# Three ordering products of a lattice stretch, moved from one quadrant of the array to three

## The chip, the core and the metric

The kernel runs on one core of a Trainium2 chip. The metric is the device time of one execution in microseconds; of the kernel before there are three timed runs, 12310.65, 12336.9 and 12346.97 us, with the median 12336.9 us. The engines that matter here are TensorE (PE in the profile; its weight loads have a row of their own, PEld), VectorE (DVE), ScalarE (ACT), GpSimd (POOL), and the DMA queue that SyncE (SP) issues.

## The reference, cut to what matters

The input x is 32 images of 8 channels of 256 by 256 values, fp32. Layer 0 normalises each image over groups of two channels and then computes three things from the result: a coupled map lattice, a small cellular network and a gate that blends the two. Layer 1 is a quantised 3x3 convolution. Each layer is added to its input. The lattice, which the change touches, is this part:

```python
drive = x[:, :C_OUT]
grid = drive
for _ in range(STEPS):                       # STEPS = 15
    mapped = R * grid * (1.0 - grid)         # R = 3.9
    local = _conv(mapped, K_local, groups=C_OUT)   # 3x3, each channel by itself
    physics = (1.0 - EPS) * mapped + EPS * local
    grid = (1.0 - BETA) * physics + BETA * drive
cml_out = jnp.clip(grid, 0.0001, 1.0 - 0.0001)
```

The network is a 3x3 convolution from 8 to 128 channels, a relu and a 1x1 convolution back to 8 with a sigmoid. The gate is a 3x3 convolution of 24 channels to 8, a relu, a 1x1 convolution and a sigmoid. Layer 1 needs the largest absolute value of the whole normalised result before it can quantise, so nothing of it can begin until all 32 images have left layer 0.

## The kernel before, in words

Layer 0 takes the images in eight groups of four. While one group is in the lattice, its network (`nca`) runs as filler between the lattice's stretches, together with the gate (`gate`) of the group before and the normalisation (`normalise`) of the group after. The function `together` writes out the order: a piece of lattice, then filler in proportion to its estimated time. On TensorE this written order is the order of the program (`tc.manual_schedule` at L258 names that engine); the other engines are placed by the planner. After the last group, the second part of the kernel (from L913 on) does layer 1.

**The lattice.** One unit of work is one channel of the four images of a group: 8 groups of 8 channels make 64 units. A unit has 15 steps, and each step is done for two halves (two images each), which alternate. So there are 64 x 15 x 2 = 1920 calls of `half` (L480). I call what one call puts on TensorE a *stretch*. The values of one half fill all 128 partitions; a row of the image is spread over partitions and its columns are dealt out over partition groups, so that the 3x3 convolution becomes products with 64 by 64 blocks of weights. The 128 by 128 array is thus used as four quadrants. `LOW` is partitions 0 to 63 and `HIGH` 64 to 127; a quadrant is named by where its input lies and where its output goes. I write LL for LOW to LOW, HH for HIGH to HIGH (the two diagonal quadrants), LH for LOW to HIGH and HL for HIGH to LOW.

**The products of a stretch.** The half has 18 tiles, cut into four jobs of 5, 5, 4 and 4 tiles (`JOBS`, L477). Each job's sum is one PSUM bank; jobs 0 and 1 lie in the first of the two PSUM tiles `two` (L485), jobs 2 and 3 in the second. A sum has two contributions into each half of the partitions: one from a diagonal quadrant and one from an off-diagonal one. `blocks` (L487) issues two products for one job, either the two off-diagonal ones or the two diagonal ones. The loop at L501 pairs an off-diagonal call of one job with a diagonal call of another, so that four products, one in every quadrant, make a *pair of calls*, A to D:

| | off-diagonal (LH and HL) | diagonal (LL and HH) | starts or adds |
|---|---|---|---|
| A | job 1 | job 0 | starts both sums |
| B | job 3 | job 2 | starts both sums |
| C | job 0 | job 1 | adds |
| D | job 2 | job 3 | adds |

The products are fp32, and the program's one product becomes two passes on the array, each with a weight load of its own. So each quadrant sees eight passes in a stretch: two in each of A, B, C and D. In the program the diagonal calls come second, and HH comes after LL; so HH is last in each of A to D.

**The marks.** After A, after B and after C the function `mark` (L271) issues one more product, of a single column, with bf16 weights from `qw`. Its result is never read. It is written to the PSUM tile `mark`, whose pool `ps_m` (L265) has one buffer, so each mark waits until the mark before it has completed. In this kernel every mark lies in HH.

**Behind TensorE.** The DVE adds the drive to the two finished PSUM tiles (`gt`, L510: the first tile when C is done, the second when D is done) and applies the map (L520), which writes the operand of this half's next step. In one of the two layouts two edge columns are then masked on POOL (L525). In the other, two DMAs on the SP queue exchange rows between partitions (`exchange`, L469). PSUM space for stretches, network and gate comes from one pool of three double banks (`unit`, L268).

Of the kernel before, what the change touches and what calls it, by code (L numbers as in the profile page):

```python
# [109 lines left out]
def kernel(  # L110
# [17 lines left out]
    V, S, G, T = nc.vector, nc.scalar, nc.gpsimd, nc.tensor  # L128
# [19 lines left out]
    qw = cp.tile([P, 3, P], BF16, name="qw")  # L148
# [106 lines left out]
    with ExitStack() as one:  # L255
# [10 lines left out]
        LOW, HIGH = slice(0, 64), slice(64, P)  # L266

        def unit():  # L268
            return ps_u.tile([P, 2, 512], F32, name="pt", tag="pt")

        def mark():  # L271

            one_ = ps_m.tile([P, 1], F32, name="mark", tag="mark")
            T.matmul(one_[HIGH], qw[HIGH, 0, HIGH], qw[HIGH, 0, 0:1], start=True, stop=True)  # L274

        fixed = lambda shape, name, dt=F32: np_.tile(shape, dt, name=name)
        hi, lo = fixed([P, 2, 2, W], "hi", F32R), fixed([P, 2, 2, W], "lo", F32R)
# [114 lines left out]
        def lattice(g):  # L392
# [76 lines left out]
            def exchange(t):  # L469

                t = t.rearrange("p (k t) j -> p k (t j)", k=2)
                n = (NT - 1) * (NJ + 2)
                above, below = slice(0, n), slice(NJ + 2, NJ + 2 + n)
                nc.sync.dma_start(t[0::16, :, below], t[14::16, :, above])
                nc.sync.dma_start(t[15::16, :, above], t[1::16, :, below])
# [4 lines left out]
            def half(c, step, s, d, m_a, m_b):  # L480

                a2b = (step + s) % 2 == 0
                n = NJ + 1 if a2b else NJ
                k = 0 if a2b else 1
                two = [unit(), unit()]  # L485

                def blocks(j, diagonal, first):  # L487
                    t0, t1 = JOBS[j]
                    pt = two[j // 2][:, j % 2, : (t1 - t0) * n].rearrange("p (t j) -> p t j", j=n)
                    own = m_a[:, t0:t1, 1 : 2 + NJ] if a2b else m_b[:, t0:t1, 0:NJ]  # L490
                    beside = m_a[:, t0:t1, 0 : 1 + NJ] if a2b else m_b[:, t0:t1, 1 : 1 + NJ]
                    if diagonal:
                        parts = ((LOW, LOW, k, own), (HIGH, HIGH, k, own))
                    elif a2b:
                        parts = ((LOW, HIGH, k, own), (HIGH, LOW, 2, beside))
                    else:
                        parts = ((HIGH, LOW, k, own), (LOW, HIGH, 2, beside))
                    for src, dst, w, rhs in parts:
                        T.matmul(pt[dst], lw[src, c, w, dst], rhs[src], start=first, stop=not first)  # L499

                for o, dg, first in ((1, 0, True), (3, 2, True), (0, 1, False), (2, 3, False)):  # L501
                    blocks(o, False, first)
                    blocks(dg, True, first)
                    if (o, dg) != (2, 3):
                        mark()

                gts = []
                for pt, (ts, w) in zip(two, HALVES):
                    gt = gp.tile([P, 10 * (NJ + 1)], F32, name="gt", tag="gt")[:, : 2 * w * n]
                    V.scalar_tensor_tensor(  # L510
                        gt.rearrange("p (u c) -> p u c", u=2), pt[:, :, : w * n], FLOOR,
                        d[:, ts, :].rearrange("p (u t) j -> p u (t j)", u=2), ALU.max, ALU.add,
                    )
                    gts.append(gt.rearrange("p (t j) -> p t j", j=n))
                for gt, (ts, w) in zip(gts, HALVES):
                    if step == STEPS - 1:
                        V.tensor_scalar(d[:, ts, :], gt, 0.0001, 1.0 - 0.0001, ALU.max, ALU.min)
                        continue
                    to = m_b[:, ts, :] if a2b else m_a[:, ts, 1 : 1 + NJ]
                    V.scalar_tensor_tensor(to, gt, 1.0, gt, ALU.subtract, ALU.mult)  # L520
                if step == STEPS - 1:
                    return a2b
                if a2b:
                    edge = m_b[:, :, 0 : NJ + 1 : NJ]
                    G.tensor_tensor(edge, edge, junk.unsqueeze(1).to_broadcast([P, TU, 2]), ALU.mult)  # L525
                else:
                    exchange(m_a)
                return a2b
# [7 lines left out]
            for c in range(C):  # L536
                u = g * C + c
                for step in range(STEPS):
                    if step == 7 and u + 1 < NG * C:
                        units[u + 1], dmas = load(u + 1)  # L540
                        later.extend(dmas)
                    if step == STEPS - 1:
                        background(len(later))
                    for s in range(2):
                        d = units[u][s][1 if (step + s) % 2 == 0 else 0]
                        a2b = half(c, step, s, d, m_a[s], m_b[s])
                        if step == STEPS - 1:
                            for k in range(2):
                                later.extend(store(g * GB + 2 * s + k, c, "b" if a2b else "a", d, k))
                            if u + 1 in units:  # L550
                                begin(units[u + 1], s)
                        background(4)
                        yield 2.05
# [359 lines left out]
    with ExitStack() as two:  # L913
# [92 lines left out]
        for b in range(B + 1):  # L1006
# [5 lines left out]
            if last:  # L1012
                i, os_ = last
                yi = ys.pop(i)
                for h, (h0, h1) in enumerate(HALVES):
                    o = os_[h][:, : h1 - h0, :]
# [61 lines left out]
```

## Time and profile before

| | before |
|---|---|
| median of three runs | 12336.9 us |
| the profiled execution, its own time | 12344.86 us |
| span in the profile | 12343.1 us |
| mean granted TensorE clock | 0.95 |
| PE busy | 11018.7 us (89%) |
| DVE busy | 7823.5 us (63%) |
| ACT busy | 3787.1 us (31%) |
| POOL busy | 1577.6 us (13%) |
| mean share of the DMA engines' time, 65 to 11378 us | 0.67 |
| first and last lattice product start | 64 us, 11379 us |
| marks | 5760, median 163 ns; their weight loads, median 107 ns |

The profile is of one execution. The span runs from its first to its last instruction. In rows of groups and of the timeline, a line such as L499 is a line of the kernel, the tile names stand as output<-inputs, "64*64" is the part of the array in use, x a count, and what stands after <- in brackets is what ended the engine's idle time. In the timeline neighbouring instructions of one kind are merged: a row's first number is the start of the first of those that touch the asked window, the second the time from there to the end of the last. The end of a matmul is modelled; it lies after the moment at which the next one in the same quadrant can start.

### The profile page before, as it was taken

How to read it: one execution, taken by the hardware profiler on the slowest of the kernel's cores; microseconds unless marked ns; L12 is line 12 of the kernel's file. 1: busy time of each engine (PE TensorE's matmuls, PEld its weight loads, DVE VectorE, ACT ScalarE, POOL GpSimd, SP SyncE). 2: the span in 40 equal slices, each digit the busy share in tenths (PEclk: the TensorE clock that was granted, in tenths of full speed). 3: DMA queues.
4: the chain of work that ended last, by engine and by line, in shares of the span. 5: the costliest groups of instructions: out<-in, count | busy, mean ns of one | idle time of the engine just before them, and what ended most of it. 6: DMA issues, size and time to landing. Idle time of an engine off the chain costs nothing. (4 is left out here: it accounts for less than half of the span.)

```text
span 12343.1 us, 289997 instructions
## 1 busy us (share of the span) xinstructions
PE 11018.7 (89%) x124192; PEld 6195.1 (50%) x124192; DVE 7823.5 (63%) x11376; ACT 3787.1 (31%) x4034; POOL 1577.6 (13%) x2242
## 2 busy tenths in 40 slices
PE   4888899999999999999999999999999999999854
PEld 2554555555555555555555555555555555555222
DVE  4555666666666666666666666666666666665377
ACT  2222233332333333333333333333333333332133
POOL 1000011111111111111111111111111111111300
PEclk7999999999999999999999999999999999999676
DMA  6545567766777667676776667677667666665988
GB/s 169 98 96 100 102 136 144 144 137 139 142 145 147 137 135 147 144 144 130 147 147 139 133 140 148 135 144 148 134 142 149 137 132 126 125 121 115 201 246 257
DMA packets 2473159, 1759.74 MB, mean 143 GB/s; under 512 B 1021280, under 2 KB 2442944, under 8 KB 2471744
## 3 DMA queue, kind: packets, MB, share of 16 engines
q1 hardware_dynamic: 2380096, 1651.64, 65.1%
q10 hardware_dynamic: 91776, 89.53, 2.3%
q8 instruction: 979, 16.04, 0.6%
q14 instruction: 308, 2.52, 0.1%
HBM read 1130.62 MB, written 473.89 MB: 130 GB/s over the span
## 5 line engine op out<-in xcount | busy, mean ns | idle before, releaser
L593 ACT ACTIVATE h<-pt,bp_sb 128x1024 f32<-128x1024 f32 x2048 | 2274.2, 1112 | 5042.4 <-PE pt L585 5032.7
L499 PE MATMUL pt<-m_a,lw 64*64 64x325 f32 (+1 forms) x30720 | 2404.9, 432 | 405.2 <-DMA m_a<-m_a 358.0
L585 PE MATMUL pt<-im,wp_hi 48*128 48x512 f32 x12288 | 2627.7, 424 | 144.7 <-ACT h L593 105.2
L510 DVE SCALAR_TENSOR_TENSOR gt<-pt,d_b 128x650 f32<-128x650 f32 (+1 forms) x1920 | 1463.6, 763 | 1987.5 <-PE mark L274 1350.7
L510 DVE SCALAR_TENSOR_TENSOR gt<-pt,d_a 128x640 f32<-128x640 f32 (+1 forms) x1920 | 1446.9, 754 | 1608.5 <-PE mark L274 1137.5
L585 PE MATMUL pt<-im,wp_lo 48*128 48x512 f32 x12288 | 2437.3, 393 | 0.0
L499 PE MATMUL pt<-m_b,lw 64*64 64x320 f32 (+1 forms) x30720 | 2305.8, 417 | 111.8 <-DVE gt L510 79.6
L499 PEld LDWEIGHTS pt<-m_a,lw 64*64 64x64 f32 x30720 | 1459.6, 137 | 1193.0 <-issue 511.4
L499 PEld LDWEIGHTS pt<-m_b,lw 64*64 64x64 f32 x30720 | 1380.3, 133 | 903.0 <-issue 451.6
L585 PEld LDWEIGHTS pt<-im,wp_hi 48*128 48x128 f32 x12288 | 1160.8, 185 | 1250.9 <-issue 730.9
L520 DVE SCALAR_TENSOR_TENSOR m_a<-gt 128x640 f32<-128x640 f32 (+1 forms) x1792 | 1429.2, 798 | 58.6
L520 DVE SCALAR_TENSOR_TENSOR m_b<-gt 128x650 f32<-128x650 f32 (+1 forms) x1792 | 1384.3, 774 | 100.6 <-DVE gt L510 1.8
L525 POOL TENSOR_TENSOR m_b<-m_b,junk 128x36 f32<-128x36 f32 x896 | 243.5, 272 | 8070.3 <-DVE m_b L520 5355.6
L585 PEld LDWEIGHTS pt<-im,wp_lo 48*128 48x128 f32 x12288 | 1166.4, 186 | 201.1
L601 PE MATMUL acc<-h,wu_z 128*32 128x512 f32 x8192 | 1107.0, 611 | 0.0
L764 PE MATMUL pt<-gin,gw 96*32 96x384 f32 (+2 forms) x10240 | 775.6, 452 | 197.2 <-ACT gate L716 181.2
L274 PE MATMUL mark<-qw 64*64 64x1 bf16 x5760 | 946.4, 164 | 0.0
L764 PE MATMUL pt<-gnc,gw 48*32 48x384 f32 (+2 forms) x10240 | 735.3, 430 | 0.0
L764 PEld LDWEIGHTS pt<-gin,gw 96*32 96x32 f32 x10240 | 313.3, 115 | 823.7 <-issue 422.0
L687 POOL TENSOR_TENSOR d<-mix 128x256 f32<-128x256 f32 x512 | 554.2, 1099 | 1254.1 <-DVE gate L722 866.6
L274 PEld LDWEIGHTS <-qw 64*64 64x64 bf16 x5760 | 631.5, 110 | 137.0 <-issue 0.6
L764 PEld LDWEIGHTS pt<-gnc,gw 48*32 48x32 f32 x10240 | 295.0, 109 | 423.0 <-issue 416.3
(110 smaller groups left out, 5940.8 us busy)
## 6 DMA issues: line engine op xcount, KB each, us to landing
im<-xp_s SPq DMA_DIRECT2D x1024, 384.0 KB
gin<-gs_s SPq DMA_DIRECT2D x512, 384.0 KB
mix<-gs_s SPq DMA_DIRECT2D x512, 384.0 KB
gnc<-gs_s SPq DMA_DIRECT2D x256, 384.0 KB
d_a<-gs_s SPq DMA_DIRECT2D x2048, 36.0 KB
yb<-y_s ACTq DMA_DIRECT2D x28, 2432.0 KB
xr<-in_x_dram SPq DMA_DIRECT2D x128, 512.0 KB
xp_s<-hi SPq DMA_DIRECT2D x256, 256.0 KB
```

The costliest lines, as they stand in the source:

```text
L274: T.matmul(one_[HIGH], qw[HIGH, 0, HIGH], qw[HIGH, 0, 0:1], start=True, stop=True)
L499: T.matmul(pt[dst], lw[src, c, w, dst], rhs[src], start=first, stop=not first)
L510: V.scalar_tensor_tensor(gt.rearrange("p (u c) -> p u c", u=2), pt[:, :, : w * n], FLOOR, d[:, ts, :].rearrange("p (u t) j -> p u (t j)", ...
L520: V.scalar_tensor_tensor(to, gt, 1.0, gt, ALU.subtract, ALU.mult)
L525: G.tensor_tensor(edge, edge, junk.unsqueeze(1).to_broadcast([P, TU, 2]), ALU.mult)
L585: T.matmul(ph[:, i, :].rearrange("p (h w) -> p h w", w=W), w[64 * i : 64 * i + 48, dx, :], rhs[:, :, dx : dx + W], start=(dx == 0 and w is ...
L593: S.activation(h.rearrange("p i c -> p (i c)"), ph.rearrange("p i c -> p (i c)"), AF.Relu, bias=bp_sb)
L601: T.matmul(acc[32 * g : 32 * g + 32], wu_z[:, 24 - 8 * i : 56 - 8 * i], hs[4 * g + i], start=(i == 0), stop=(i == 3),)
L687: G.tensor_tensor(d[:, cols], mix[:, 1, k], mix[:, 2, k], ALU.subtract)
L764: T.matmul(three[32 * i : 32 * i + 32, :, to], gw[:rows_, j, dx, :], src[:, i::4, of], start=(j == 0 and n == 0), stop=(j == 1 and n == le ...
```

## The change

The mark gets a number, 0 to 2, and each number has its own quadrant: mark 0 stays in HH, mark 1 lies in LL and mark 2 in LH. Place in the program, size, operand tile and the waits on the mark tile are as they were, and so are all other products.

```diff
-        def mark():
-
+        MARKS = ((HIGH, HIGH), (LOW, LOW), (LOW, HIGH))
+
+        def mark(n):
+
+            src, dst = MARKS[n]
             one_ = ps_m.tile([P, 1], F32, name="mark", tag="mark")
-            T.matmul(one_[HIGH], qw[HIGH, 0, HIGH], qw[HIGH, 0, 0:1], start=True, stop=True)
+            T.matmul(one_[dst], qw[src, 0, dst], qw[src, 0, 0:1], start=True, stop=True)
@@ half @@
-                for o, dg, first in ((1, 0, True), (3, 2, True), (0, 1, False), (2, 3, False)):
+                for n_, (o, dg, first) in enumerate(((1, 0, True), (3, 2, True), (0, 1, False), (2, 3, False))):
                     blocks(o, False, first)
                     blocks(dg, True, first)
-                    if (o, dg) != (2, 3):
-                        mark()
+                    if n_ < len(MARKS):
+                        mark(n_)
```

## The prediction

> **What bounds the kernel now.** I read the page's busy times and slices first, then who PE waited for, then one stretch of the lattice in the timeline.
>
> ```profile
> PE 11018.7 (89%) x124192; PEld 6195.1 (50%) x124192; DVE 7823.5 (63%) x11376; ACT 3787.1 (31%) x4034; POOL 1577.6 (13%) x2242
> ...
> PE   4888899999999999999999999999999999999854
> ```
>
> PE is at 90% or more in nearly every slice that holds lattice work; no other engine comes near. The lattice runs from 64 to 11379 us. Next, PE's waits:
>
> ```profile
> PE pt L499 <- DMA m_a<-m_a: 358.0, 144, 12.0
> ...
> PE pt L764 <- ACT gate L716: 181.2, 222, 0.9
> PE pt L585 <- ACT h L593: 105.2, 85, 2.0
> PE pt L499 <- DVE gt L510: 92.8, 90, 4.8
> ```
>
> The columns are total us, times, longest. The largest, the wait for the row exchange, happens at 144 of 1920 stretches. All waits of PE together are under a tenth of the lattice's 11313 us. So PE's program order, one thing after another, sets the time there, and a nanosecond taken off a stretch is mostly a nanosecond off the end.
>
> Now one stretch in the 65-column layout, from 6019.11 to 6021.42 us, when the next filler product starts: 2.31 us. I asked for PE in windows so narrow that single passes show. First, three windows in order of time, just after each mark has started; the x1 rows are a product of HH alone:
>
> ```profile
> 6019.73 0.16 PE L274 MATMUL mark<-qw 64*64 64x1 bf16 x1
> 6019.76 0.41 PE L499 MATMUL pt<-m_a,lw 64*64 64x260 f32 x1
> ...
> 6020.23 0.16 PE L274 MATMUL mark<-qw 64*64 64x1 bf16 x1
> 6020.26 0.46 PE L499 MATMUL pt<-m_a,lw 64*64 64x325 f32 x1
> ...
> 6020.83 0.16 PE L274 MATMUL mark<-qw 64*64 64x1 bf16 x1
> 6020.86 0.41 PE L499 MATMUL pt<-m_a,lw 64*64 64x260 f32 x1
> ```
>
> After each mark the HH product starts 0.03 us later (0.028 in the records). And here is the end of the stretch, at two moments close together:
>
> ```profile
> 6020.92 0.57 PE L499 MATMUL pt<-m_a,lw 64*64 64x260 f32 x4
> ...
> 6021.11 0.38 PE L499 MATMUL pt<-m_a,lw 64*64 64x260 f32 x1
> ...
> 6021.42 0.50 PE L585 MATMUL pt<-im,wp_hi 48*128 48x512 f32 x2
> ```
>
> The x4 row is the last pass of all quadrants: three of them begin at 6020.92 and within 14 ns. The x1 row is the last pass of HH: 6021.11. HH is some 0.19 us behind LH, and the next work starts only when HH is through. The cause stands in the weight loads:
>
> ```profile
> 6019.71 0.21 PEld L499 LDWEIGHTS pt<-m_a,lw 64*64 64x64 f32 x5
> 6020.01 0.11 PEld L274 LDWEIGHTS <-qw 64*64 64x64 bf16 x1
> ```
>
> The load for mark 1 starts at 6020.01, when HH's second pass of B starts (the other quadrants' started at 6019.93); it takes the place in which HH's next weights could have been loaded ahead.
>
> **What the skill says.** "TensorEngine Tiling (Array Packing)", Key Properties: tiles of one mode work independently, and a change of the mode drains the engine. The trace agrees with both: HH falls behind while three quadrants go on, and the filler waits for HH. The same page, Instruction Overhead, says that a one-column product costs about what 60 columns cost. In "TensorE: Matmul & The Clock Gate", LDWEIGHTS, a load costs columns / 1.2 ns, so an estimate of 53 ns for 64 columns when nothing hides it. The trace below gives 58. Part 3 of that page, The mechanism, says that matmuls start strictly in program order. The trace differs, and decides: in the records the first LH pass of C, which follows mark 1 in the program, starts 78 ns before mark 1, and that of D 137 ns before mark 2.
>
> **The change, costed.** Nothing is added or removed: three loads and three one-column products a stretch, as now. Two of them leave HH.
>
> *What a mark costs its quadrant.* The median records of the 65-column stretch, in ns after its first product. HH: mark 0 at 618, first pass of B 646, second 895; mark 1 at 1114, C at 1143 and 1446; mark 2 at 1719, D at 1748 and 1997. LL, which has no mark: B at 611 and 830, C at 1049 and 1323, D at 1596 and 1815. HH is issued 7 ns behind LL. So HH is late by 895 - 830 - 7 = 58 after mark 0, by 1446 - 1323 - 7 = 116 after mark 1, by 1997 - 1815 - 7 = 175 after mark 2: 58 each time. Of these, 28 lie between the mark and the next product, and 30 in that product's own length (249 instead of 219), because its load could not begin before the mark did. In the 64-column layout it is 1970 - 1791 - 6 = 173, the same 58 a mark.
>
> *After the change.* HH carries mark 0 alone: 58. LL carries mark 1: 58, from C on. LH carries mark 2: 58, in D. HL carries none. The three end together: in the 65-column layout the last passes start at 1802 + 58 = 1860 (LH), 1815 + 58 = 1873 (LL), 1997 - 117 = 1880 (HH). So the stretch ends 116 ns earlier: 2 x 58. Times 1920 stretches: 222.7 us, which is the full gain in PE's order.
>
> The trace of before has no mark outside HH. Its cost in LL or LH can't be below nothing, and at nothing the gain would be the same, since HH keeps its own 58; above 58 each ns is lost from the gain, up to the 232 of the slower rival. I take 58: the quadrants' loads and passes have the same lengths.
>
> *The waits.* Each mark waits for the one before it, and behind it on PE stand all products of the next pair. Mark 1 starts in LL at 1049, not 1114, and mark 2 in LH at 1582 (when LH is through C), not 1719: so neither wait is met later than now. The DVE waits for C and for D of HH; those come 58 and 116 ns earlier. The DMAs, POOL and the SP queue get no instruction more.
>
> *What is given back.* Where PE stands still for something of fixed length, a shorter stretch in its cover makes the wait longer. Stalls of the lattice and the network by the list of PE's waits: 144 for the exchange, 85 + 21 for ACT's relu, 90 + 22 for the DVE: 362. Each can take back at most the 116 ns of one stretch: 42 us; I take half, 21, because in the exchange's chain the own stretch is shortened too. The gate's 222 waits follow directly on gate products with no stretch between in the timeline that I read, and so are unchanged. The DVE (63%) hides its own work as before; if its cover went, PE would wait at the next step of the same half. That slack is large: between POOL's masking of an operand and the stretch that uses it lie over 3.1 us in 19 of 20 cases.
>
> Sum: 222.7 - 21 = 202 us. The profiled execution took 12344.9 us, which is 8 above the median of 12336.9; against the median the forecast is 12136 us (-1.6%). Within this case: nothing given back gives 12114, all 42 gives 12156.
>
> **The rivals.**
>
> *One of the two marks gains nothing.* LH (and, in the other layout, HL then LH) stands first in each pair. If a load or product that waits for mark 2's place holds back those behind it in the program, all four quadrants pay 58 in D. LL and HH are already 58 late there, which should hide it, but if it does not they end 116 late, and half the gain is left: 111 us, less 10: 12236. For it: the loads of C start in a row at 1015 ns in the stretch shown, just behind mark 1's load at 1011, although three quadrants were free from 931 on; so something there kept order. Against: they overtake in A to B, where B's loads began at 441 and mark 0's at 461.
>
> *No change.* The 58 ns could belong to PE and not to a quadrant, or HH be late for being last in the order. Against it: three quadrants run through without a break while HH alone slips, at each mark by the same 58. It would give 12337.
>
> *Slower.* Mark 2 in LH blocks the queue until it has run, and the loads behind it then go one after another with nothing to hide them: four times 58 = 232, plus HH's 58 from mark 0: 290 behind where it is 175 now. That is 115 ns a stretch more, +221 us: 12558. It decides once more than three loads in a row are exposed. Against it: four loads of one pair start 6 to 7 ns apart (113 to 133 in the stretch shown) and overlap.
>
> **How the numbers follow.** Chances: full gain 0.74, half gain 0.17, no change 0.04, slower 0.05. A measurement of this kernel tells about 0.3% (37 us) from no change. Faster, by the first two: 0.91; within 0.3%: 0.04; slower: 0.05. The range runs from just under the full gain with nothing given back, 12105, to just over the half gain, 12240.
>
> **What would show it.** In the timeline, HH alone should be late after mark 0 only (28 ns behind it), LL after mark 1, LH after mark 2; a stretch should take 2.19 us where it took 2.31; the last passes of LH, LL and HH should start within some 20 ns of each other. The loads of B, C and D should still begin ahead of their products. PE's waits should grow by 0 to 42 us. The prediction is wrong if HL, which has no mark, is late in D; if the other quadrants wait for the one with the mark; or if the stretches shorten and the wait for the exchange or for ACT takes it back.

## The result, and the profile after

The changed kernel takes 12252.81 us in the median of four runs (12231.09 to 12266.57); the kernel before, 12333.86 us. The ratio is 0.9935, with a 95% interval of 0.9912 to 0.9958: 81 us faster, where some 200 were forecast. The time lies 13 us outside the forecast range. In a second measurement (`e7_after_again`, below) the ratio was 0.9925 (0.9912 to 0.9937), 93 us.

The page of the changed kernel, its busy times; the profiled execution took 12231.09 us, its span 12229.3:

```profile
PE 10809.9 (88%) x124192; PEld 6033.0 (49%) x124192; DVE 7826.2 (64%) x11376; ACT 3791.0 (31%) x4034; POOL 1577.2 (13%) x2242
```

PE has 209 us less to do than before, and yet the span of the profiled executions shrank by 114 only. The same stretch as in the prediction (the 1003rd of 1920), in the timeline of PE. First the marks, then three narrow windows near the end:

```profile
5981.54 0.16 PE L277 MATMUL mark<-qw 64*64 64x1 bf16 x1
5981.57 0.41 PE L502 MATMUL pt<-m_a,lw 64*64 64x260 f32 x1
...
5981.97 0.16 PE L277 MATMUL mark<-qw 64*64 64x1 bf16 x1
...
5982.51 0.16 PE L277 MATMUL mark<-qw 64*64 64x1 bf16 x1
...
5982.73 0.45 PE L502 MATMUL pt<-m_a,lw 64*64 64x260 f32 x4
...
5982.78 0.40 PE L502 MATMUL pt<-m_a,lw 64*64 64x260 f32 x3
...
5983.11 0.50 PE L588 MATMUL pt<-im,wp_hi 48*128 48x512 f32 x2
```

The stretch began at 5980.92 and the filler starts at 5983.11: 2.19 us instead of 2.31. The x4 row is the last pass of all quadrants, from HL at 5982.73 on; once HL is through, the x3 row remains, LH from 5982.78 with LL and HH 13 and 20 ns behind it. No quadrant is 0.19 us behind LH any more. The median 65-column stretch has its last passes at 1860 (LH), 1873 (LL) and 1880 ns (HH): to the nanosecond what the prediction worked out. The part of the forecast that says what the change does to a stretch held in full.

The waits of PE, in the columns of before:

```profile
PE pt L502 <- DMA m_a<-m_a: 410.1, 153, 12.3
...
PE pt L767 <- ACT gate L719: 178.0, 218, 0.9
PE pt L588 <- ACT h L596: 116.6, 84, 2.1
PE pt L502 <- DVE gt L513: 96.4, 92, 5.5
...
PE pt L588 <- DVE gt L513: 24.7, 72, 1.5
```

The wait for the exchange grew from 358.0 to 410.1 us and came 153 times instead of 144; in the profile of the second measurement it took 401.9 us in 144 times. The gate's is unchanged, as predicted. The network's wait for the DVE (last row) came 72 times in both. Before, it was:

```profile
PE pt L585 <- DVE gt L510: 13.7, 22, 1.4
```

**Where the rest went.** I took the time between each two neighbouring products in the records, from the first lattice product to the last, and compared it with what the same two kinds take when nothing disturbs them (the lower quartile of the kind). What lies over it is a wait, or the clock at half rate. In us, after minus before, for the two profiled executions of the changed kernel:

| | first profile | second profile |
|---|---|---|
| undisturbed work of PE | -222 | -230 |
| waiting for the exchange (m_a) | +49 | +40 |
| waiting for ACT's relu (h) | +16 | +15 |
| waiting for the DVE (gt) | +13 | +19 |
| products at half the clock | +26 | +65 |
| others | +11 | +10 |
| lattice, first to last product | -106 | -82 |

The undisturbed work fell by 222 us, the forecast's full gain. More than half of it came back, in three places: the exchange, the two waits for PSUM space that ACT and the DVE give free, and the clock. The rows are good to some microseconds, but for the clock's. When the kinds are told apart more finely, by the place in the stretch too, undisturbed work falls by 223 and 227 us and the clock's row is 20 and 50.

**The clock.** TensorE spends 659 us of the lattice at half the clock before, and 720 and 765 us after, in 100 episodes before and 112 and 126 after. More runs point the same way: taken beside each other, nine runs of before had a mean granted clock of 0.9502 and five of the changed kernel 0.9470. With two clocks, full and half, that makes some 70 us more at half, as an estimate.

The Trainium skill, "TensorE: Matmul & The Clock Gate", What's actually happening, says that the clock falls to half after an idle window of about 3.4 us. The records agree in the unit: nearly all episodes last 3.4 us or two to four times that. They do not need a whole idle window: in the 6.8 us ahead of an episode PE stood still for 2.1 to 2.3 us in the median, and in 87 of the 100 episodes of before no single stall had reached 3.4 us when the clock fell. A 65-column stretch that lies wholly in an episode takes 3.87 us from first to last pass where it takes 1.997 otherwise (medians of before). Of the 144 waits for the exchange before, 57 had an episode begin during them or within 3.4 us after them (64 of 153 and 71 of 144 in the two profiles of the changed kernel), and none began inside one. Such a stall is paid twice, once by its length and once by the slow products behind it.

### The profile page after: what moved, and what is told of

The parts are those of the page before. It is cut to its first block, busy times and chain, and to the rows that moved or that the text cites. A ratio compares the mean times of both kernels' runs of the same rounds, so it can differ in the third digit from the quotient of the medians.

```text
span 12229.3 us, 289998 instructions
## 1 busy us (share of the span) xinstructions
PE 10809.9 (88%) x124192; PEld 6033.0 (49%) x124192; DVE 7826.2 (64%) x11376; ACT 3791.0 (31%) x4034; POOL 1577.2 (13%) x2242
## 5 line engine op out<-in xcount | busy, mean ns | idle before, releaser
L502 PE MATMUL pt<-m_a,lw 64*64 64x325 f32 (+1 forms) x30720 | 2299.3, 433 | 464.9 <-DMA m_a<-m_a 410.1
L502 PE MATMUL pt<-m_b,lw 64*64 64x320 f32 (+1 forms) x30720 | 2200.5, 417 | 118.1 <-DVE gt L513 82.1
L502 PEld LDWEIGHTS pt<-m_a,lw 64*64 64x64 f32 x30720 | 1316.6, 138 | 1193.2 <-issue 596.9
L502 PEld LDWEIGHTS pt<-m_b,lw 64*64 64x64 f32 x30720 | 1237.4, 134 | 858.4 <-issue 463.5
L767 PE MATMUL pt<-gnc,gw 48*32 48x126 f32 (+2 forms) x10240 | 733.1, 429 | 0.0
```

The source lines that it names most:

```text
L767: T.matmul(three[32 * i : 32 * i + 32, :, to], gw[:rows_, j, dx, :], src[:, i::4, of], start=(j == 0 and n == 0), stop=(j == 1 and n == le ...
```

## The experiments

The theory after the result: part of the program is not set by PE's order but by turns of a chain (a stretch up to the end of C, the DVE, the exchange, the next stretch of the same half). There, what a stretch loses comes back as a wait. The rivals: a toll for marks in several quadrants; waits that grow only because the kernel had just about enough slack; ACT, the DVE and PSUM instead of the exchange.

**Mark 1 alone moved, and mark 2 alone moved.** Both take one mark out of HH and shorten the stretch equally.

```diff
-        MARKS = ((HIGH, HIGH), (LOW, LOW), (LOW, HIGH))
+        MARKS = ((HIGH, HIGH), (LOW, LOW), (HIGH, HIGH))    # first run
+        MARKS = ((HIGH, HIGH), (HIGH, HIGH), (LOW, HIGH))   # second run
```

> Part of the change alone: mark 1 lies in LL, marks 0 and 2 in HH. HH should be 116 ns late at the end of a stretch and the 65-column stretch take 2.25 us (2.306 before, 2.190 after). If the time given back comes evenly with every ns taken off (give-back in chains that do not shrink), the gain is half of the change's: about 40 us, ratio 0.9967. If a fixed toll is paid for having marks in different quadrants (rival), the gain is much under half: 0 to 15 us. If the conversion is good at first and gets worse with the depth of the cut (rival), it is over 65 us of the 111 us in the order.

> Only mark 2 leaves HH (for LH). As in the run that moved only mark 1, HH ends a stretch 116 ns late and the stretch takes 2.25 us; but HH is now late by 116 ns at the end of C too, as in the kernel before, where that run had 58. The DVE starts at the end of C, so the way from the last product of a stretch to the finished operand should be 2.994 us (2.936 in before, 3.002 after). If that chain counts, the gain is smaller than that run's 44 us: 20 to 40 us. If only the length of the stretch counts (rival), it is the same 44 us.

With mark 1 moved: 12279.69 us against 12323.67, ratio 0.9964 (0.9949 to 0.9979), 44 us. With mark 2 moved: 12308.94 against 12334.17, ratio 0.9981 (0.9968 to 0.9995), 25 us. In both, the 65-column stretch has its last pass at 1938 ns, 59 less than before. So no toll shows: half of the cut brings about half of the gain, of the 111 us in PE's order 40% with mark 1. With mark 2 it is 23%, which is the direction that the chain predicts; but the two intervals overlap, so the difference is not settled.

What the records do show is the chain itself, in the 64-column stretches, whose next operand is the one that is exchanged. From the start of a stretch's last pass to the end of the DVE's last write of the operand it takes 2.936 us before, 2.945 with mark 1 moved, 2.993 with mark 2 moved and 3.002 with both (medians). From the stretch's first pass, that is 4.907, 4.857, 4.906 and 4.858 us: moving mark 1 makes the chain 50 ns shorter, and moving mark 2 leaves it as it was. Here is the DVE's first operation behind the stretch shown, before and after. That stretch is of the 65-column layout, whose next operand is masked and not exchanged, but the DVE begins in the same way:

```profile
6021.03 0.83 DVE L510 SCALAR_TENSOR_TENSOR gt<-pt,d_b 128x650 f32<-128x650 f32 x1 [0.25 <-PE pt L499]
```

```profile
5982.79 0.84 DVE L513 SCALAR_TENSOR_TENSOR gt<-pt,d_b 128x650 f32<-128x650 f32 x1
```

The stretch began at 6019.11 before and at 5980.92 after, so the DVE begins 1.92 and 1.87 us into it. It starts when C is done, and then has four operations in a row, some 3 us, to the finished operand. Its way is shorter by some 50 ns, near C's 58, and not by the stretch's 116.

**The marks doubled.**

```diff
             T.matmul(one_[HIGH], qw[HIGH, 0, HIGH], qw[HIGH, 0, 0:1], start=True, stop=True)
+            T.matmul(one_[HIGH], qw[HIGH, 0, HIGH], qw[HIGH, 0, 0:1], start=True, stop=True)
```

> The disputed cost doubled: each mark of the kernel before is issued twice, all in HH. HH should end a stretch some 350 ns late instead of 175, so 1920 stretches put up to 336 us more into TensorE's order. If waits of fixed length swallow about half of what a stretch changes by, in both directions, the kernel is 130 to 180 us slower; if waits grow when the stretch shrinks but there was little to give when it grows (rival), it is 280 us or more slower.

12401.42 us against 12323.67, ratio 1.0057 (1.0042 to 1.0072): 78 us slower by the medians, 70 by the ratio. This is under both expected ranges. The second mark cost less than the first: the last pass starts at 2092 ns instead of 1997, 95 more for three marks, where 175 were expected. That is 182 us in PE's order, and 43% of it appears by the medians (39% by the ratio). PE's wait for the exchange shrank:

```profile
PE pt L500 <- DMA m_a<-m_a: 286.1, 116, 11.1
```

So the share of about four tenths holds in both directions. The kernel before was not at an edge of its slack: for longer stretches as for shorter ones, more than half of the change is taken up on the way.

**Without the exchange.** In the kernel before and in the changed one:

```diff
-                else:
-                    exchange(m_a)
```

> The kernel before with the exchange of rows between partitions left out (the two DMAs of the layout that needs them; rows at the borders of the tiles then miss their neighbours). The waits of PE for m_a (358 us in the profile before) should go, and with them part of the half clock: 300 to 420 us faster than before, 11.9 to 12.0 ms.

> The changed kernel, also with the exchange left out. If the exchange is what takes the gain back (first theory), this is 165 to 200 us faster than the kernel before without the exchange. If ACT, the DVE and PSUM space take it back (rival), the distance between the two stays at 70 to 120 us.

12044.76 us and 11882.61 us: 162 us apart by the medians (by their ratios to before, 0.9771 and 0.9642, it is 0.0129 of 12323.67, 159 us). Both come out slightly under what was expected: before without the exchange is 279 us faster than before (300 to 420), and the distance was to be 165 to 200. Without the exchange 73% of the 222 us arrive. The exchange therefore stands behind roughly the half of what was missing, 162 - 81 = 81 us (69 by the second measurement; the distances are known to some 15 to 30 us), more than the 40 to 49 us by which its own wait grew; the clock goes with it: the time at half rate in the lattice is 515 and 522 us here, nearly the same. What remains moves into ACT's relu and the DVE. The waits of the two kernels, before's first:

```profile
PE pt L583 <- ACT h L591: 133.2, 89, 4.4
PE pt L499 <- DVE gt L510: 103.1, 96, 5.6
```

```profile
PE pt L586 <- ACT h L594: 158.8, 93, 5.1
...
PE pt L502 <- DVE gt L513: 110.1, 94, 5.1
```

**Without the network's image loads.** Why is the exchange late? It is issued at once: its first DMA starts on SP 0.064 us after the DVE's last write, in the median of the stretches that then wait for it just as in the others. From the end of the issue to the waiting stretch's start it takes 4.5 us in the median and up to 9.6 (nine in ten). The next pair of runs takes away 400 of the 1760 MB that the kernel moves, which lowers the share of the DMA engines' time that SP's queue takes from 65.1% to 41.9%.

```diff
             im = ims[(NT8 * b + t) % 2]
+            if NT8 * b + t >= 2:
+                return im
```

> The kernel before without the loads of the network's images after the first two (the network then works on stale values; 1024 large DMAs are left out, all the rest stays). If the exchange is late because the DMA engines are busy with such loads (first theory), PE's wait for m_a falls from 358 us to under 150 us and the kernel is 150 to 300 us faster. If the exchange's own latency makes the wait (rival), it stays above 250 us.

> The changed kernel without those loads. First theory: with the exchange on time, the marks' move is worth 140 to 180 us (distance to the kernel before without the loads). Rival: it stays at 70 to 100 us.

12142.52 us and 12028.94 us. In the kernel before the wait for the exchange falls to a third, so these loads, by their bytes or by their place in the queue, make it late:

```profile
PE pt L499 <- DMA m_a<-m_a: 123.5, 68, 7.2
```

```profile
PE pt L502 <- DMA m_a<-m_a: 133.2, 80, 9.3
PE pt L502 <- DVE gt L513: 116.1, 116, 3.6
...
PE pt L590 <- DVE gt L513: 63.0, 86, 4.2
```

But the distance between the two kernels is 114 us, under the 140 to 180 of the theory and over the 70 to 100 of the rival, and with some 25 us of uncertainty it is below the theory's range but not clear of the rival's. The exchange takes back only 10 us here; by the account used above, the DVE's waits take 39, ACT's relu 16 and slowed products 34 (15 by the finer account; the time at half rate, 567 and 543 us, did not grow, so this row is not settled). With one chain relieved, more of the loss lies in the next one.

**The exchange, or the loads, on another queue.** All work is done in these.

```diff
-                nc.sync.dma_start(t[0::16, :, below], t[14::16, :, above])
+                nc.gpsimd.dma_start(t[0::16, :, below], t[14::16, :, above])    # and its twin
...
-                    nc.sync.dma_start(
+                    nc.scalar.dma_start(                                        # loads of im, other run
                         im.bitcast(F32)[64 * q : 64 * q + 48, k, :, 1 : 1 + W],
```

> The kernel before with the two exchange DMAs issued on POOL's queue instead of SP's; nothing is left out. If the exchange lands late because it stands behind the large loads in SP's queue (first theory), PE's wait for m_a falls from 358 us to under 100 us and the kernel is 150 to 300 us faster than before. If it is late because all DMA engines are busy, whatever the queue, or because an issue on POOL is itself slow (rival), the wait stays above 300 us and the time is that of before or worse.

> The changed kernel with the exchange on POOL's queue. First theory: with the wait gone the marks' move is worth 140 to 190 us (distance to the kernel before with the exchange on POOL's queue), as it was 162 us without any exchange. Rival (the engines' bandwidth): the distance stays near 80 us.

> The changed kernel with the network's image loads issued on ACT's queue, the exchange still on SP's; nothing is left out. If the exchange waits in line behind those loads in its own queue, the wait for m_a falls under 250 us (400 to 410 in the changed kernel) and the kernel gains 60 to 200 us on it. If the DMA engines as such are busy (rival), the wait stays above 330 us and the time within 40 us of the changed kernel, or above it because ACT now stops for the loads' buffers.

None of the three went as the first theory had it; in the first and the third the wait and the time did what the rival said, and in the second neither side's distance came. With the exchange on POOL's queue: 13158.18 and 13032.98 us, 6.6% and 5.6% slower than before. With the loads on ACT's: 12929.91 us, 4.9% slower. The waits for the exchange grew in each. Of the first and the third:

```profile
PE pt L499 <- DMA m_a<-m_a: 869.8, 307, 9.0
```

```profile
PE pt L502 <- DMA m_a<-m_a: 577.9, 209, 8.4
PE pt L767 <- ACT gate L719: 331.2, 220, 10.4
```

In the first, one pair of issues keeps POOL busy for 1.13 us (573 + 557 ns), and the exchange begins 0.54 us after the operand is ready instead of 0.06. In the third, ACT must stop for the loads' buffers, and the gate that it computes comes later too (178 us of waiting in the changed kernel). Neither relieves the exchange by leaving the line in SP's queue. But each also gives another engine more to do, so whether it is that queue or the DMA engines' load as such that delays it stays open. The two POOL kernels stand 125 us apart, between the 140 to 190 of the theory and the 80 of the rival.

**The changed kernel again**, beside these:

> The changed kernel again, on the chip of the two runs beside it: 70 to 95 us faster than before, ratio 0.9925 to 0.9945.

12251.36 us against 12344.19, ratio 0.9925 (0.9912 to 0.9937), 93 us. The changed kernel is the fastest of the kernels here that compute everything.

## Why the prediction was right and wrong

- *What a mark costs its quadrant, and that it costs the same in LL and LH:* right. Some 58 ns each, 2.19 us a stretch, the three quadrants' last passes within 20 ns. 222 us less undisturbed work.
- *The waits of the marks, and the order in PE's queue:* right. HL, without a mark, is not late, and nothing was held back behind mark 2. The half-gain rival has nearly the measured time (12236) for a wrong reason: its place was the order in the array, and there all of the gain arrived.
- *What is given back:* wrong, and this is the step that failed. It was put at 21 us and at 42 at most. The waits alone took 80 to 90 us and the clock another 20 to 65. It failed in three ways. First, the bound of "the 116 ns of one stretch" per stall: at the 122 stretches that waited for the exchange both before and after, the wait grew by 194 ns in the median (170 at 123 stretches in the second profile). One turn of a half holds two stretches, 231 ns less in all (117 and 114), and the chain itself became only 49 ns shorter; the difference, 182 ns, is near what was measured. The same sum gives 66 ns with mark 1 moved, where the median is 72, but 115 with mark 2 moved, where it is 79. The single waits scatter by far more than this (the middle half of the 122 from -159 to +736 ns), so the sum is supported and not proven. Second, "in the exchange's chain the own stretch is shortened too" halved the sum, although the same text said that the DVE waits for C, and C came only 58 ns earlier. Third, stalls were counted as they stood: the network's for the DVE rose from 22 to 72, and 31 stretches waited for the exchange that had not before, while 22 no longer did.
- *The clock:* missing from the sum. The prediction priced a longer wait at its length. With the longer waits came 61 and 106 us more at half the clock, which the two accounts price at 20 to 65 us.
- *PE's program order sets the time there, "mostly a nanosecond off the end":* too much was read from PE's busy share. With under a tenth of the lattice spent waiting, the share of a cut that arrives was still only four tenths.
- *The sign, and the slower rival:* faster, as forecast; no sign of loads in a row with nothing to hide them.
- *Slips that change nothing:* the terms of the sum give 12135, not 12136. And where the prediction has 441, 461, 931, 1011, 1015 and 113 to 133 ns for the stretch shown, it counts from 6019.000 us; its medians count from a stretch's first product, which here is at 6019.115.

What stays open: how the loss divides between the exchange and the clock, since the two go together, there is one profile of before, and the clock's part differed between two profiles of the same changed kernel (26 and 65 us); and what exactly makes the exchange late.

## What to carry to other kernels

A busy engine at 90% does not tell what a cut in its work will bring. Double the cost in question and time it: here the doubled marks showed 39 to 43% of what they put into PE's order, and moving two of them brought 36 to 42% of what that took out. For each stall in the way, ask where its chain starts, and by how much that point moves; it is not the end of the piece that became shorter. On TensorE add what the slowed clock costs behind the stalls that set it off.

## What the runs showed of the hardware that was not expected

- A second one-column product in the same quadrant, right behind the first, cost 32 ns (95 for three), where the first costs 58.
- The clock fell to half after 2.1 to 2.3 us of standing still within 6.8 us, in the median; in 87 of 100 episodes no single stall had reached 3.4 us by then.
- A row exchange of 33 KB a DMA, issued within 0.064 us in the median, was used 4.5 us after its issue in the median of the stretches that waited for it; without the network's loads, 400 MB, the number of such stretches fell from 144 to 68.
